# Two state-space layers on one core: gates between the convolution's products, bias as a weight row, other PSUM rooms, later weight loads

## The chip, the cores and the metric

The kernel runs on one core of one Trainium2 chip. The metric is the device time of one execution, in microseconds (us). The kernel before takes 1482.97 us, the median of three runs (1477.59 to 1486.76). A core has TensorE (PE in the profile), VectorE (DVE), ScalarE (ACT), GpSimd (POOL) and SyncE (SP). Each takes its own instructions in order and waits for the others by semaphores. All DMAs here but a few are issued by SP, one after another.

## The reference, cut to what matters

An image of 64x64 tokens with 96 channels goes through two layers. Each normalizes its input over groups (`_gn`), computes a branch and adds it to its input. The second layer reads (the first is built the same way, without a separate projection per direction):

```
xz = x @ in_proj_w.T                    # 96 -> 384
xin, z = jnp.split(xz, 2, axis=-1)      # 192 channels each
xc = conv 3x3, depthwise, SAME (xin)
u  = silu(xc + conv_b)
y  = four selective scans of u (rows and columns, both ways), summed
y  = layernorm(y)
y  = y * silu(z)                        # the gate
return y @ out_proj_w.T
```

The scan's recurrence is `h = h * exp(dt*A) + dt*u*B`, its output `sum over the states of h*C` plus `D*u`. Each layer has 192 channels and 16 states per channel.

## The kernel before, in words

The main loop (L1712 to L1746) runs over the two layers. It loads the layer's weights (`scan_weights`, L186, and L1714 to L1724), calls `head`, then the scans, then a tail which normalizes, gates, projects and adds. Layer 1's scans are `near_scans` (L267): there the state dies out so fast that short stretches suffice. A flag computed on the chip decides whether `far_scans` (L606, inside `tc.If`) has to run; in the profiled execution it didn't. Layer 2's scans are `scans` (L724); in the trace all their operations bear the line L738. Everything before their steady run is in `first` (L995).

The 192 channels are three tiles of 64. A tile lies on 128 partitions, as two halves: the upper 64 partitions hold the even groups of 512 tokens (8 image rows), the lower 64 the odd ones. So `u[T]` is 128x2048, and a chunk `c` (0 to 3) is 128x512. `HALF` names the two halves.

`head(l, xT, w)` (L1252) computes `u` and the gate. Its parts:

- *Normalization.* The statistics `st` of the input are aggregated (`bn_aggr`), averaged over groups by a product with `gav` (the results go to `small`, columns at the end of the PSUM tile `accs`), and turned into a factor `rs` and a `shift`. DVE scales the weights by `rs` into `ws`; nine tiny products of weights and `shift` (`offset`) give the bias of every channel, copied to `bias`.
- *In-projections.* `project(b, c)` makes the 128x512 of tile `b` and chunk `c` by two products of 64 columns of weights with 512 tokens. `padded` (L1323) copies it with ACT, bias added, into `pad[b]`, an image with a border of one pixel. `borders(b)` (L1330) is four DMAs on SP that fill the rows above and below each chunk from the other half (the halo).
- *Convolution.* The twelve pieces (3 tiles, 4 chunks) are split over the engines. PE does tile 2's chunks 0 to 2 (`tap_pe`, nine products with diagonal matrices into a sum `cp`). DVE does three pairs of chunks (`tap_dve`, nine multiply-adds of 128x1052 in PSUM; a sum has 1056 floats, and two of them stand alternately in `accs`, a tile of five PSUM banks). ACT multiplies (`tap_act`) and POOL adds (`tap_pool`) for three more chunks. `silu` (ACT) turns a finished sum into `u`.
- *Gates.* `gate01` multiplies 128 columns of weights at once, for tiles 0 and 1; `gated01` is the SiLU by ACT, followed by two DMAs of 128 KB, as a 128x512 result holds two tiles. `gate2` and `gated2` do tile 2, with one DMA of 256 KB. The results wait in DRAM (`szd`) until the tail.
- *Start of y.* `start_y` (L1249, POOL here) sets `y = ds * u`, six pieces of 128x1024.

The PSUM of in-projections, `cp` sums and gates is a pool of three rooms of one bank. The SBUF pool of the gate results `sz` has four buffers.

The order inside the head is written by hand: each step gets a due time (`at`, L1423 to L1473), and the steps are issued in order of these times. Instructions issued through the helper `Ordered` (recorded as L261 in the head) keep that order on their engine; those issued through `nc` may be moved by the compiler's scheduler. In the head's PE order the in-projections come first, then the 27 products of `cp`, then the twelve gate units. Between, the due times on ACT alternate pad copies, tap products and SiLUs:

```
        for c in range(3):
            for k in range(9):
                at(t + 0.9 * k, tap_pe, 2, c, k)
            t += 8.1
            at(t + 0.1, silu, 2, slice(HT * c, HT * (c + 1)), partial(whole, ("cp", c)))
        for g in range(8):
            at(t, gate01, g)
            at(t + 0.5, gated01, g)
            t += 0.5
```

On SP, layer 1's head has, besides halos and gate stores, layer 2's weights: five loads of `ipw`, `v`, `op`, and 44 of `scan_weights(1)` for its second pair of directions, issued from 37.64 us on (those of the first pair follow the near scans). After the head, layer 2's `first` has on POOL's queue the loads of `du` (`spread`, L947) and a share of the products `bT`; `pj` is its first product, `xd` its copy by ACT.

Of the kernel before, what the change touches and what calls it, by code (L numbers as in the profile page):

```python
# [9 lines left out]
F32 = mybir.dt.float32  # L10
BF16 = mybir.dt.bfloat16
AF = mybir.ActivationFunctionType
ALU = mybir.AluOpType
# [4 lines left out]
HW = 64  # L18
# [26 lines left out]
def two_ss2d_layers(  # L45
# [107 lines left out]
    xT = xp.enter_context(tc.tile_pool(name="xT0", bufs=1)).tile([DM, L], F32, name="xT0")  # L153
# [32 lines left out]
    def scan_weights(l):  # L186

        xw, dwb, am = [], [], []  # L190
        D = 1 + l
        for p in range(1 + l):
            lp = 2 * l + p
            w = swp.tile([128, 2, 3, NC], F32, tag=f"xw{p}", name=f"xw{lp}")
            v = swp.tile([128, 2, 3, 128], F32, tag=f"dwb{p}", name=f"dwb{lp}")
            e = swp.tile([128, 2, 3, NS + 1], F32, tag=f"ab{p}", name=f"ab{lp}")
            a = swp.tile([128, 2, 2, 3, NP], F32, tag=f"am{p}", name=f"am{lp}")
            nc.vector.memset(v[96:128, 0:D], 0.0)
            for d in range(D):
                r = slice(NB + RK * d, NB + RK * d + RK)  # L200
                rr = slice(RK * d, RK * d + RK)
                hi = slice(64 * d, 64 * d + 64)
                c0 = NB + 2 * RK + NS * d
                for half in HALF:
                    for to, of in ((slice(0, NC - NS), slice(0, NC - NS)), (slice(NC - NS, NC), slice(c0, c0 + NS))):
                        nc.sync.dma_start(
                            out=w[half, d, 0:2, to],
                            in_=xpw[lp, :, d, of].rearrange("(b p) c -> p b c", b=2),
                        )
                        nc.sync.dma_start(out=w[half, d, 2, to], in_=xpw[lp, hi, 2, of])  # L210
                    nc.sync.dma_start(
                        out=v[r, d, 0:2, half], in_=dtw[lp, rr, d, :].rearrange("r (b p) -> r b p", b=2)
                    )
                    nc.sync.dma_start(out=v[r, d, 2, half], in_=dtw[lp, rr, 2, hi])
                    for b, (of, q) in enumerate(((HALF[0], d), (HALF[1], d), (hi, 2))):
                        nc.sync.dma_start(
                            out=v[NC : NC + 1, d, b, half],
                            in_=alb[lp, of, q, NS : NS + 1].rearrange("p o -> o p"),
                        )
                    nc.sync.dma_start(  # L220
                        out=e[half, d, 0:2, :],
                        in_=alb[lp, :, d, :].rearrange("(b p) n -> p b n", b=2),
                    )
                    nc.sync.dma_start(out=e[half, d, 2, :], in_=alb[lp, hi, 2, :])
            xw.append(w)
            dwb.append(v)
            am.append((a, e, D))
        return xw, dwb, am
# [38 lines left out]
    def near_scans(weights):  # L267
# [5 lines left out]
        with ExitStack() as sc:  # L273
# [25 lines left out]
            )  # L299

# [278 lines left out]
            weights_of(1)  # L579
            for j in range(len(units)):  # L580
                if j > 1:
                    weights_of(j)
                if 0 < j < len(units) - 1:
                    operands(j + 1)
                scan(j)
                if j == 1:
                    reach()
                if j == 2:
                    reached()
                if j == 4:  # L590
                    sum_up(1)
                add(j)
                if j == 3:
                    sum_up(0)
# [129 lines left out]
    def scans(weights, pps, ready):  # L724
# [18 lines left out]
        with ExitStack() as sc:  # L743
# [251 lines left out]
            def first(  # L995
# [3 lines left out]
                parts = [delta(T) for T in range(3)]  # L999
                for h in range(2):  # L1000
                    project(h)
# [250 lines left out]
    def head(l, xT, w):  # L1252

        ipw_s, v, ds = w["ipw"], w["v"], w["ds"]
        with ExitStack() as sc:
# [16 lines left out]
            gm, rs, shift = gst[:, 2:3], gst[:, 5:6], gst[:, 6:7]  # L1272
            dve.bn_aggr(gst[:, 0:2], w["st"].rearrange("p a b -> p (a b)"))
            W2 = HW + 2
            accs = cvp.tile([128, 5 * HT], F32, name=f"accs{l}")
            small = accs[:, 4 * SR * W2 : 4 * SR * W2 + 8]
# [10 lines left out]
            ws = cv.tile([DM, 2 * DI], F32, name=f"ws{l}")  # L1287
            bias = cv.tile([128, 5], F32, name=f"bias{l}")
            dve.scalar_tensor_tensor(shift, gm, -1.0, rs, ALU.mult, ALU.mult)
            for cut in (slice(0, 64), slice(64, DI), slice(DI, 2 * DI)):  # L1290
                dve.tensor_scalar_mul(ws[:, cut], ipw_s[:, cut], rs)

            def offset(to, of, n):
                pe.matmul(
                    small[to, 2 + n : 3 + n], ipw_s[:, of : of + to.stop - to.start], shift,
                    start=True, stop=True,
                )

            for half in HALF:
                offset(half, 0, 0)  # L1300
            for n in (1, 2):
                for half in HALF:
                    offset(half, 64 * n, n)
            offset(slice(0, 128), DI, 3)
            for half in HALF:
                offset(half, DI + 128, 4)
            dve.tensor_copy(bias, small[:, 2:7])
# [3 lines left out]
            def room(name):  # L1311
                return cvp.tile([128, HT], F32, tag="in", name=name, bufs=3)

            def project(b, c):
                ps = live["in", b, c] = room(f"in{l}_{b}_{c}")
# [7 lines left out]
            def padded(b, c):  # L1323
                act.activation(
                    pad[b][:, c, 1 : SR + 1, 1 : HW + 1],
                    live.pop(("in", b, c)).rearrange("p (r w) -> p r w", w=HW),
                    AF.Identity, bias=bias[:, b : b + 1],
                )
# [11 lines left out]
            def gate01(g):  # L1340
                ps = live["z", g] = room(f"z{l}_{g}")
                pe.matmul(
                    ps, ws[:, DI : DI + 128], xT[:, g * 512 : (g + 1) * 512], start=True, stop=True
                )

            def gated01(g):
                c, h = divmod(g, 2)
                sz = cw.tile([128, HT], F32, tag="sz", name=f"sz{l}_{g}")
                act.activation(sz, live.pop(("z", g)), AF.Silu, bias=bias[:, 3:4])
                for b, half in enumerate(HALF):  # L1350
                    sp.dma_start(
                        out=szd[l][b, HALF[h], HT * c : HT * (c + 1)], in_=sz[half]
                    )

            def gate2(c):
                ps = live["z2", c] = room(f"z{l}_2_{c}")
                for h, half in enumerate(HALF):
                    g = 2 * c + h
                    pe.matmul(
                        ps[half], ws[:, DI + 128 : 2 * DI], xT[:, g * 512 : (g + 1) * 512],  # L1360
                        start=True, stop=True,
                    )

            def gated2(c):
                sz = cw.tile([128, HT], F32, tag="sz", name=f"sz{l}_2_{c}")
                act.activation(sz, live.pop(("z2", c)), AF.Silu, bias=bias[:, 4:5])
                sp.dma_start(out=szd[l][2, :, HT * c : HT * (c + 1)], in_=sz)
# [19 lines left out]
            def tap_pe(b, c, k):  # L1387
                if k == 0:
                    live["cp", c] = room(f"cp{l}_{b}_{c}")
# [6 lines left out]
            def tap_dve(n, b, c, k):  # L1396
                i, j = taps[k]
                o = i * W2 + j
                acc = accs[:, 2 * SR * W2 * (n % 2) :][:, 0 : 2 * SR * W2]
                live["acc", b, c] = acc.rearrange("p (c r w) -> p c r w", r=SR, w=W2)  # L1400
# [26 lines left out]
            for b, order in ((0, (2, 3, 1, 0)), (2, (3, 2, 1, 0)), (1, (3, 2, 1, 0))):  # L1427
                for c in order:
                    at(t, project, b, c)
                    at(t + 0.95, padded, b, c)  # L1430
                    t += 0.9
                at(t + 1.0, borders, b)
            for c in range(3):
                for k in range(9):
                    at(t + 0.9 * k, tap_pe, 2, c, k)
                t += 8.1
                at(t + 0.1, silu, 2, slice(HT * c, HT * (c + 1)), partial(whole, ("cp", c)))
            for g in range(8):
                at(t, gate01, g)
                at(t + 0.5, gated01, g)  # L1440
                t += 0.5
            for c in range(NCH):
                at(t, gate2, c)
                at(t + 0.9, gated2, c)
                t += 0.9
            t = 2.6
            for n, (b, c) in enumerate(((0, 2), (0, 0), (1, 0))):
                for k in range(9):
                    at(t, tap_dve, n, b, c, k)
                    t += 1.3  # L1450
                at(
                    t + 0.1, silu, b, slice(HT * c, HT * (c + 2)),
                    lambda b=b, c=c: live.pop(("acc", b, c))[:, :, :, 0:HW],
                )
            t = 7.4
            for b, c in ((2, 3), (1, 3), (1, 2)):
                for k in range(9):
                    at(t - 1.5, tap_act, b, c, k)
                    if k:
                        at(t, tap_pool, b, c, k)  # L1460
                        t += 1.3
                at(
# [363 lines left out]
```

## Time and profile before

| what | us |
|---|---|
| runs, median of 3 | 1482.97 |
| profiled execution, its own time | 1485.29 |
| its span | 1483.5 |
| head of layer 1, from `bn_aggr` to the first `nu` product | 18.7 to 83.5 |
| near scans, to DVE's last sum | 83.5 to 153.5 |
| tail of layer 1, to the first `bn_aggr` of layer 2 | 156.2 to 199.6 |
| head of layer 2, to the first `pj` product | 199.6 to 258.5 |
| layer 2's first DVE product `b*du` | 287.1 |

The mean TensorE clock granted is 0.932. How to read the profile: the page's first lines give each engine's busy time, its share of the span and the number of instructions. Then the span is cut into 40 slices, and each digit is a share in tenths. The chain is the work that ended last, followed back from the end, by engine and by line. A row of the timeline is start, duration, engine, line, operation, output <- input, shapes, count, and in brackets how long the engine had been idle and who released it; a row with a count over one spans several instructions. A row of the waits is who waited for whom: us in total, times, longest. An fp32 product is recorded as two passes, so `x54` is 27 products.

### The profile page before, as it was taken

Reading aid. Unit: us, or ns where it says so; the run is one execution under the profiler, and the core shown is the slowest. Engines: PE = TensorE matmul, PEld = TensorE weight load, DVE = VectorE, ACT = ScalarE, POOL = GpSimd, SP = SyncE. Lnnn points to the kernel's source line nnn. Section 1 sums busy time; section 2 is a strip of 40 time slices with the busy share of each in tenths; the row PEclk is TensorE's granted clock in tenths of the full one; section 3 lists DMA queues with packets and bytes.
Section 4 is the critical chain, followed back from the end, with each engine's and each line's share of the span. In section 5 each row is a group of like instructions: output and inputs, shape, how many; then the busy total and the mean of one; then the engine's idle time right before and its main releaser. Section 6 shows DMA issues by size and latency. Waiting matters only on the chain.

```text
span 1483.5 us, 17337 instructions
## 1 busy us (share of the span) xinstructions
PE 1222.3 (82%) x5047; PEld 480.5 (32%) x5047; DVE 1317.1 (89%) x909; ACT 1224.9 (83%) x2508; POOL 1205.4 (81%) x663
## 2 busy tenths in 40 slices
PE   6874879598888888888797989798988888886888
PEld 3333323233332323333333333333333333322333
DVE  4738576579999999999999999999999999999996
ACT  5765347679989988999999999999998889897873
POOL 1843018679999998989898989898989898989895
PEclk9965879689899999999999999999999999999999
DMA  3251522615352626262626262626262626262634
GB/s 109 45 123 26 145 50 61 160 31 124 77 136 65 146 65 149 57 157 58 145 57 144 58 144 59 143 59 143 59 142 59 142 59 150 61 147 67 146 87 127
DMA packets 85812, 147.70 MB, mean 100 GB/s; under 512 B 33692, under 2 KB 36956, under 8 KB 85612
## 3 DMA queue, kind: packets, MB, share of 16 engines
q1 hardware_dynamic: 84028, 143.96, 40.7%
q0 software_dynamic: 576, 1.57, 0.4%
q8 instruction: 41, 0.67, 0.2%
q10 hardware_dynamic: 1104, 0.98, 0.2%
q14 instruction: 63, 0.52, 0.1%
HBM read 80.85 MB, written 12.13 MB: 63 GB/s over the span
## 4 chain that ended last, share of the span: by engine, by line
DVE 30%; issue 23%; PE 10%; ACT 10%; POOL 7%; DMA 6%; SPq 2%; DVEq 0%; POOLq 0%; ACTq 0%
DVE h L738 19%; DVE b L738 8%; POOL hc L738 5%; ACT a L738 3%; PE ys L738 3%; ACT bT L738 2%; PE pj L738 2%; DMA cb<-C 2%; PE b L738 2%; SPq L738 2%; DVE accs L261 1%; DMA szt<-szd 1%; DMA xT<-xs 1%; DMA du<-su 1%; PE pd L738 1%
## 5 line engine op out<-in xcount | busy, mean ns | idle before, releaser
L738 POOL TENSOR_TENSOR hc<-h,cb 128x1024 f32<-128x1024 f32 x384 | 903.5, 2373 | 94.1 <-DVE h L738 41.5
L738 DVE TENSOR_TENSOR_SCAN h<-a,carry,b 128x1024 f32<-128x1024 f32 x288 | 664.6, 2337 | 26.2 <-PE b L738 3.5
L738 ACT ACTIVATE a<-dt,am 128x1024 f32<-128x1024 f32 x384 | 438.3, 1142 | 69.3 <-DVE h L738 63.2
L738 PE MATMUL ys<-hc,fold 128*64 128x512 f32 x1536 | 430.0, 639 | 0.3 <-POOL hc L738 0.2
L738 ACT ACTIVATE bT<-duT,BT 128x192 f32<-128x192 f32 x1012 | 387.3, 445 | 3.6 <-PE b L738 1.3
L738 PE MATMUL b<-ident,bT 128*128 128x128 f32 x1536 | 219.4, 286 | 26.4 <-DVE h L738 18.2
L738 DVE TENSOR_TENSOR b<-b,du 128x1024 f32<-128x1024 f32 x192 | 231.9, 1208 | 6.8 <-PE b L738 6.8
L738 DVE TENSOR_TENSOR_SCAN h<-a,b 128x1024 f32<-128x1024 f32 x96 | 216.3, 2278 | 12.7 <-POOL hc L738 2.5
L738 PE MATMUL b<-B,selh 96*128 96x512 bf16 x384 | 117.2, 387 | 131.4 <-DVE h L738 131.2
L738 PEld LDWEIGHTS b<-ident,bT 128*128 128x128 f32 x1536 | 174.4, 145 | 150.9 <-DVE h L738 90.8
L738 PEld LDWEIGHTS ys<-hc,fold 128*64 128x64 f32 x1536 | 77.7, 138 | 141.2 <-issue 106.2
L738 PEld LDWEIGHTS <-selh 96*128 96x128 bf16 x384 | 25.6, 98 | 258.7 <-DVE h L738 204.4
L261 POOL TENSOR_TENSOR tap<-tap,tap 128x512 f32<-128x512 f32 x48 | 61.0, 1273 | 47.8 <-ACT tap L261 45.0
L738 PE MATMUL pj<-u,xw 64*124 64x512 f32 x192 | 94.1, 635 | 1.9 <-DVE w L738 1.2
L261 DVE SCALAR_TENSOR_TENSOR accs<-pad,v,accs 128x1052 f32<-128x1052 f32 x48 | 63.3, 1319 | 12.7 <-DMA pad<-pad 6.3
L738 PE MATMUL ys<-y,ident 128*128 128x512 f32 (+1 forms) x120 | 61.2, 612 | 0.0
L738 ACT CAST B<-pj 96x512 bf16<-96x512 f32 (+2 forms) x96 | 54.9, 575 | 4.7 <-PE pj L738 4.7
L738 POOL TENSOR_TENSOR sp<-sp,ln 128x512 f32<-128x512 f32 x45 | 57.8, 1284 | 0.2
L738 POOL TENSOR_TENSOR ln<-ln,w 128x512 f32<-128x512 f32 x45 | 57.9, 1286 | 0.0
L738 POOL TENSOR_TENSOR su<-sp,u 128x512 f32<-128x512 f32 x45 | 57.7, 1282 | 0.0
L261 POOL MEMSET pad<- 128x40 f32 (+1 forms) x24 | 2.7, 170 | 67.0 <-DVE g L1524 51.1
L738 PE MATMUL pd<-xd,dwb 29*64 29x512 f32 x192 | 55.0, 646 | 0.0
(184 smaller groups left out, 1234.9 us busy)
## 6 DMA issues: line engine op xcount, KB each, us to landing
cb<-C SPq DMA_DIRECT2D x256, 256.0 KB
dt<-sp SPq DMA_DIRECT2D x192, 128.0 KB
du<-su SPq DMA_DIRECT2D x180, 128.0 KB
szt<-szd SPq DMA_DIRECT2D x24, 256.0 KB
szd<-sz SPq DMA_DIRECT2D x32, 128.0 KB
xT<-xs SPq DMA_DIRECT2D x8, 384.0 KB
szd<-sz SPq DMA_DIRECT2D x8, 256.0 KB
xs<-xT SPq DMA_DIRECT2D x1, 1536.0 KB
```

What stands on the lines that cost most here:

```text
L261: return lambda *args, **more: tc.keep_in_program_order(op(*args, **more))
L738: return lambda *args, **more: tc.keep_in_program_order(op(*args, **more))
```

## The change

1. `xT` gets a 97th row of ones (a POOL memset). The bias becomes the 97th row of the weights `ws`: one product of a 96x97 matrix `low` (zero but for its last column, the shift) with the weights, and a copy of one row. The nine `offset` products and the bias copy go. The pad copies are plain copies, two of the twelve by DVE.
2. The three rooms become two of one bank, by name: in-projections alternate by chunk, `cp` sums take room 0, gates room 1. DVE's sums get three banks of their own each, two of them.
3. Gates are twelve units (tile, chunk) of two products, each stored by one DMA of 256 KB; `sz` has eight buffers. The units stand between the `cp` products: 39 slots, nine of each thirteen for `cp`.
4. DVE, ACT and POOL do the first three taps of two pieces (the row that needs no halo) before the other taps of the first.
5. `start_y` moves from the head to the near scans (POOL, behind its memsets and `picked`) and to layer 2's `first`, ahead of POOL's `du` loads and `bT` products there.
6. Layer 2's `ipw`, `v`, `op` and the scan weights of its second pair of directions (49 DMAs) are issued in the near scans, behind the copies of `nS` on SP and ahead of its last loads `ab` and the branch. The sum `ds` of layer 2 goes with them (DVE).

```diff
-    xT = ....tile([DM, L], F32, name="xT0")
+    xT = ....tile([DM + 1, L], F32, name="xT0")
+    nc.gpsimd.memset(xT[DM : DM + 1], 1.0)
+    ones, xT = xT, xT[0:DM]
...
+    def layer_weights(l, queue):
+        w = {"st": st[l], "next": st[1]}
+        w["ipw"] = wts.tile([DM, 2 * DI], F32, name=f"ipw{l}")
+        queue.dma_start(out=w["ipw"], in_=ipw[l])
...
+        nc.vector.reduce_sum(w["ds"], v[:, :, V_D : V_D + 4], axis=AX.X)
+        return w
...
-    def near_scans(weights):
+    def near_scans(weights, later):
...
+            for start in later:
+                start()
...
             weights_of(1)
+            look_ahead()
...
                 parts = [delta(T) for T in range(3)]
+                for start in later:
+                    start()
                 for h in range(2):
                     project(h)
...
-            accs = cvp.tile([128, 5 * HT], F32, name=f"accs{l}")
-            small = accs[:, 4 * SR * W2 : 4 * SR * W2 + 8]
+            def room(name, tag):
+                return cvp.tile([128, HT], F32, tag=f"p{tag}", name=name)
+            small = room(f"pm{l}", 0)
...
-            for half in HALF:
-                offset(half, 0, 0)
...
-            dve.tensor_copy(bias, small[:, 2:7])
+            ws = cv.tile([DM + 1, 2 * DI], F32, name=f"ws{l}")
+            low = cv.tile([DM, DM + 1], F32, name=f"low{l}")
+            pool.memset(low, 0.0)
+            dve.scalar_tensor_tensor(low[:, DM:], gm, -1.0, rs, ALU.mult, ALU.mult)
+            offset = room(f"of{l}", 1)[0 : DM + 1, 0 : 2 * DI]
+            pe.matmul(offset, low, ipw_s, start=True, stop=True)
+            dve.tensor_scalar_mul(ws[0:DM], ipw_s, rs)
+            dve.tensor_copy(ws[DM:], offset[DM:])
...
-            def room(name):
-                return cvp.tile([128, HT], F32, tag="in", name=name, bufs=3)
...
-                act.activation(
+                copy = dve.tensor_copy if (b, c) in ((0, 2), (0, 1)) else act.copy
+                copy(
...
+            def gate(b, c):
+                ps = live["z", b, c] = room(f"z{l}_{b}_{c}", 1)
...
+                        ps[half], ws[:, DI + 64 * b : DI + 64 * b + 64],
+                        xT[:, g * 512 : (g + 1) * 512], start=True, stop=True,
...
+            def gated(b, c):
+                sz = cw.tile([128, HT], F32, tag="sz", name=f"sz{l}_{b}_{c}", bufs=8)
+                act.activation(sz, live.pop(("z", b, c)), AF.Silu)
+                sp.dma_start(out=szd[l][b, :, HT * c : HT * (c + 1)], in_=sz)
...
-                    live["cp", c] = room(f"cp{l}_{b}_{c}")
+                    live["cp", c] = room(f"cp{l}_{b}_{c}", 0)
...
+                if k == 0:
+                    live["acc", b, c] = cvp.tile(
+                        [128, 3 * HT], F32, tag="acc", name=f"acc{l}_{b}_{c}", bufs=2
+                    )[:, 0 : 2 * SR * W2]
...
+            for n in range(39):
+                c, k = divmod(n * 9 // 13, 9)
+                if n * 9 % 13 < 9:
+                    at(t, tap_pe, 2, c, k)
+                    if k == 8:
+                        at(t + 1.0, silu, 2, slice(HT * c, HT * (c + 1)), partial(whole, ("cp", c)))
+                else:
+                    z = n - (n * 9 // 13 + 1)
+                    at(t, gate, z // NCH, z % NCH)
+                    at(t + 0.95, gated, z // NCH, z % NCH)
+                t += 0.87
...
+            for b, c, k0, k1 in (
+                (0, 2, 0, 3), (0, 0, 0, 3), (0, 2, 3, 9), (0, 0, 3, 9), (1, 0, 0, 9)
+            ):
...
+            for b, c, k0, k1 in (
+                (2, 3, 0, 3), (1, 3, 0, 3), (2, 3, 3, 9), (1, 3, 3, 9), (1, 2, 0, 9)
+            ):
...
+    def look_ahead():
+        ahead["w"] = layer_weights(1, sp)
+        ahead["sw"] = scan_weights(1, 1, sp)
...
-        sw = scan_weights(l)
-        head(l, xT, w)
+        w = ahead.pop("w") if l else layer_weights(0, nc.sync)
+        sw = list(zip(*[scan_weights(l, 0, nc.sync)] + ([ahead.pop("sw")] if l else [])))
+        later = head(l, ones, w)
```

## The prediction

> **What bounds the kernel now.** I read the page first: busy shares, the 40 slices, the chain by engine and line.
>
> ```profile
> span 1483.5 us, 17337 instructions
> PE 1222.3 (82%) x5047; PEld 480.5 (32%) x5047; DVE 1317.1 (89%) x909; ACT 1224.9 (83%) x2508; POOL 1205.4 (81%) x663
> ...
> PEclk9965879689899999999999999999999999999999
> ...
> DVE 30%; issue 23%; PE 10%; ACT 10%; POOL 7%; DMA 6%; SPq 2%; DVEq 0%; POOLq 0%; ACTq 0%
> ```
>
> DVE sets the whole, but in layer 2's scans; the change doesn't touch those. The low clock digits lie in the first fifth, where the heads are, so I took the windows of the two heads, of head 0's gate stage, and of the steady scan.
>
> ```profile
> core 0: us, PE busy (x) PEld busy (x) DVE busy (x) ACT busy (x) POOL busy (x), PEclk, DMA share, GB/s
> 18.70:83.50 64.80, 56.31 (x157) 21.52 (x157) 37.54 (x38) 42.13 (x69) 41.93 (x29) 0.89 0.38 88
> 70.70:83.50 12.80, 9.73 (x21) 2.24 (x19) 0.00 (x0) 6.27 (x9) 11.58 (x6) 0.60 0.88 203
> 199.60:258.50 58.90, 52.38 (x157) 20.39 (x157) 37.46 (x37) 39.36 (x61) 36.98 (x27) 0.89 0.23 51
> 320.00:1440.00 1120.00, 952.40 (x4184) 361.13 (x4184) 1083.84 (x602) 1019.22 (x2144) 1040.94 (x514) 0.97 0.43 101
> ```
>
> Head 0 takes 64.8 us and head 1 58.9 us, and TensorE is the busiest in both. The 5.9 us between them lie in the second row: clock 0.60, DVE idle. The timeline shows why:
>
> ```profile
> 70.69 13.99 SPq L261 DMA_DIRECT2D szd<-sz  x20
> ...
> 73.80 0.69 ACT L261 ACTIVATE sz<-z,bias 128x512 f32<-128x512 f32 x1 [4.07 <-DMA szd<-sz]
> ...
> 74.54 9.01 PE L261 MATMUL z<-xT,ws 96*128 96x512 f32 x18 [3.07 <-ACT sz L261]
> ```
>
> The first gate was ready at 66.7, but its store was issued only at 70.69, since SP was at layer 2's 49 loads (37.64 to 70.69). With four `sz` buffers ACT stopped for 4.07 us; TensorE stopped behind it and came back at half rate. Head 1 has no such queue. From its timeline and table of waits:
>
> ```profile
> 220.16 24.96 PE L261 MATMUL cp<-pad,diag 128*128 128x512 f32 x54 [2.28 <-ACT pad L261]
> ...
> 258.50 3.80 PE L738 MATMUL pj<-u,xw 64*124 64x512 f32 x12
> ...
> 262.33 0.59 ACT L738 COPY xd<-pj 124x512 f32<-124x512 f32 x1 [0.38 <-PE pj L738]
> ```
>
> ```profile
> ACT sz L261 <- DMA szd<-sz: 3.6, 6, 0.8
> ...
> DVE accs L261 <- DMA pad<-pad: 3.3, 1, 3.3
> ...
> DVE accs L261 <- ACT u L261: 2.4, 2, 1.2
> ```
>
> TensorE goes from 204.08 to 258.50 and straight into layer 2's `pj`: this sets the end of the head. DVE's sums end at 250.88, so its two waits are off that path.
>
> **What the Trainium skill says.** "PSUM — Partial Sum Buffer", section "PSUM bank collisions raise a hardware error": two engines may not touch one bank (in the same partitions) at once, even at different columns, so they are ordered by bank. The trace agrees: a sum of 1056 floats reaches into the other's bank, and DVE waits 1.18 us twice for ACT's 1.11 us `u`. "TensorE: Matmul & The Clock Gate", Part 1: the array drops to half rate after an idle window of about 3.4 us. The trace shows the halves (0.86 against 0.43 us a pass), but an idle of 2.28 us already brought it (four passes of 0.86 from 220.16), while waits of 0.9 to 1.0 at 214.8 to 216.5 didn't; and after 3.07 us idle it stayed slow for 9 us. "SBUF — State Buffer", "Who interferes with whom": DVE with two SBUF inputs contends with GpSimd's reads, which bears on the moved `start_y`; layer 2's first DVE work lasted 0.69 us an instruction with GpSimd's `y` beside it (267.3 to 269) and without (271 on), so I charge nothing.
>
> **Part by part, in head 1's times.**
>
> *Bias as a weight row.* The 18 tiny passes (1.64 us) go; one product of 384 columns comes. Two passes at half rate, by the columns' ratio from 0.86: 0.64 each, 1.28, from about 202.7 to 204.0; then a row copy on DVE, 0.5 (0.56 for the 128x384 COPY). First `in` at 204.75 instead of 204.08: +0.67. The GpSimd memset of one row of 4096 isn't in the trace: from 128x384 at 0.42 and 32x768 at 0.73 I take 3.5 us (0.4 if elements across partitions counted, 7 at worst). It precedes the identity, which the transposes at 3.9 need; their next input lands at 7.1 and DVE's first statistics come at 12.3, so up to 7 is mostly hidden; kept at 0.
>
> *Two rooms instead of three for in-projections.* Freely running, TensorE would need 5.4 us for the slow start (204.08 to 209.5 now, 3.2 pairs) and 8.8 pairs at 0.86, and be through at 217.8. With two rooms it waits for the copies: about 1.0 at `in(0,1)`, and 1.65 behind `pad(2,3)`, where ACT also has tap products; through at about 220.4. `cp` takes the room of the last copy, `pad(1,0)`, while now it waited only for `pad(1,2)`: that copy ends about 222.3, so `cp` starts at 222.5 instead of 220.16: +2.3, the 0.67 in it.
>
> *Gates between the convolution's products.* 27 `cp` and 12 gate units at 0.86: 33.5 us. Now it is 27x0.86, 8x0.86 and 4x1.08 (the last paced by ACT), the half-rate start (+1.7) and waits (1.17, 0.44, 0.19, 0.26). New: all three `cp` sums share one room, so sums 2 and 3 each wait about 1.05 for the `u` before them (0.69 and two hand-overs, of which 1.17 is the sample). 222.5+33.5+2.1+0.3 = 258.4; up to 1.7 more if `cp` starts at half rate. So TensorE ends where it ended: what the denser order wins, the later start takes.
>
> *The end of the head.* `pj` takes the bank of the last `cp` sum and waits for its `u`, at 259.4 to 261.1; the second `xd` copy follows 3.8 us later (258.50 to 262.33 now): 263.2 to 264.9, +0.9 to +2.6. I take +1.9.
>
> *Whole stores, eight buffers.* 12 issues instead of 20; ACT's 3.6 us go. No gain beyond the above, since gates are now spread over 33 us.
>
> *Own banks for DVE's sums, first taps before the halo.* The 3.3 and 2.4 go, two pad copies of about 0.7 come: DVE ends near 247 instead of 250.9, GpSimd's sums stay near 252. Both lie under TensorE's 258: 0.
>
> *`start_y` moved.* Six GpSimd instructions of 2.84 us (17.06) now follow the head. In layer 2 they precede 12 `du` loads on GpSimd's queue (0.536 each, 6.4) and its four `bT` products. With last `u` at T, `y` ends T+17.1, the issues T+23.5; `bT` (284.82 now, T+26.3 moved) keeps 2 to 3 us, and the first `du` lands about 283 against its use at 289. Without this cover each further us costs one. In layer 1 `y` runs from 82 to 99; GpSimd's next use is at about 105: hidden by 6 us.
>
> *Layer 2's weights later.* The 49 loads (30.5 us without the halo among them, 0.62 each) move behind the near scans' `nS` copies and ahead of the last `ab` loads and SP's branch. SP starts them at about 111 and reaches the branch at 145; DVE's near work ends at 148 to 150 (153.48 now). Hidden by about 4; it becomes the bound if an issue costs over 0.71. Nobody in layer 1 waits for those `ab`. The small sum `ds` on DVE now stands among the near scans, behind a load that lands around its turn: +0.3.
>
> *Head 0* is the same walk 180.87 earlier: TensorE ends at 77.5 to 79.2, so the near products `nu` start 4.3 to 6.0 before 83.47: -5.1. They also start at full clock (now 4.2 us for 24 passes of 192 columns at half rate): -0.5 to -1.5, I take -0.7. With +0.3: -5.5.
>
> **Sum.** -5.5+1.9 = -3.6. The profiled execution's own time is 1485.29 (1.8 us around the span): 1481.7. The runs' median is 1482.97, so 1479.4 on that scale.
>
> **Rivals.** (A) *Both heads win.* TensorE stays at full rate through `cp`'s start, the `u` waits are covered by the gate units in between, and `pj` doesn't meet the last bank: head 1 -3, head 0 -8 with -1.5 in `nu`: -12.5, 1470.5. For: the waits of 0.9 that kept the clock. Against: one room for three sums. (B) *The other side: two rooms keep TensorE at half rate through the in-projections.* Place: `in` to `cp`. 12 pairs at 1.71 from 204.75 end 225.3, with the last waits `cp` starts at 226.9, +4.4 in each head: head 1 +6.3, head 0 -1.1, sum +5.2: 1488.2. It decides if the new waits reach the 2.28 us that brought half rate; at 1.0 they don't; 1.65 lies between. (C) *The 4.07 only moves:* ACT, TensorE or the `u` of GpSimd's sums (252) hold head 0 as before, or the branch waits for SP: sum about 0, 1483. (D) *SP or GpSimd becomes the bound:* with 0.9 us an issue SP is 44 us at it, 9 past DVE: +5.4 net, 1488; GpSimd's `y` slowed to 3.6 by DVE eats its slack and 2 us more.
>
> **Chances.** Forecast 0.48, own range 1474 to 1485 (the two ends of each term, +-2.5, and the runs' scatter of 9 us from 1477.6 to 1486.8). A 0.20, B 0.17, C 0.08, D 0.07. The range 1467 to 1491 takes in A and B with some scatter. About 1%, 14.8 us, is what a measurement of this kernel can tell from no change. Faster than 1468.1: a half of A and a little unforeseen, 0.13. Slower than 1497.8: the tails of B and D, 0.07. Same: 0.80.
>
> **What would show it.** In the changed profile: no `sz` wait for `szd` and `nu` at 77.5 to 79.5 (head 0's step); `cp` starting 2.3 later after the first `in` +0.7, with a clock digit that doesn't fall before it (against B); two waits of about 1 us of `cp` for `u`; `pj` behind the last `u`, second `xd` copy 0.9 to 2.6 later, measured from the head's `bn_aggr`; SP through with its loads before DVE's last near sum; `bT` on GpSimd not waiting for its own queue. I am wrong if TensorE's products between `cp` and the last gate take less than 33 us or more than 38, if the scan from 320 on changes its period, or if the near stage ends on SP.

## The result, and the profile after

The changed kernel takes 1497.79 us, median of 14 runs (1490.45 to 1506.71), against 1482.99 for the kernel before in its 14 runs (1477.59 to 1489.65): ratio 1.0096, 95% interval 1.0071 to 1.0121. (Ratios, here and below, are those on record for the runs, not quotients of the two medians.) It is slower by 10.5 to 18 us, where the forecast was 3.6 faster. The profiled execution (1506.71) is the longest of the 14, so I compare stages, and leave the end of layer 2's scans, which the change doesn't touch, for the last paragraph on the cause.

The page of the changed kernel:

```profile
span 1504.9 us, 17294 instructions
...
PE 1240.2 (82%) x5047; PEld 475.1 (32%) x5047; DVE 1323.0 (88%) x909; ACT 1215.3 (81%) x2504; POOL 1213.3 (81%) x667
...
PEclk8985979779889988999999999999999999999999
...
DVE 26%; issue 21%; PE 12%; POOL 11%; ACT 10%; DMA 6%; SPq 3%; DVEq 0%; POOLq 0%; ACTq 0%
```

PE and POOL have grown on the chain, DVE has shrunk, and the low clock digits are still there. The windows of the two heads, from `bn_aggr` to what follows, then two stretches inside head 1:

```profile
18.54:86.15 67.61, 59.74 (x156) 16.98 (x157) 38.63 (x37) 38.83 (x67) 32.06 (x27) 0.85 0.25 79
199.64:268.05 68.41, 59.89 (x156) 16.76 (x156) 39.55 (x38) 37.76 (x61) 30.50 (x24) 0.85 0.21 68
217.00:224.00 7.00, 5.00 (x20) 1.07 (x20) 6.82 (x7) 6.38 (x13) 4.78 (x5) 1.00 0.20 41
224.00:231.00 7.00, 6.99 (x10) 1.77 (x10) 6.86 (x6) 3.68 (x5) 4.55 (x4) 0.54 0.26 70
```

Head 0 has grown from 64.8 to 67.6 us, head 1 from 58.9 to 68.4. DMA is quiet (0.25 and 0.21): the store queue that stopped head 0 is gone, and something else has taken more. TensorE's timeline in head 1 shows what:

```profile
209.19 7.10 PE L271 MATMUL in<-xT,ws 97*64 97x512 f32 x20 [0.68 <-ACT pad L271]
217.11 3.94 PE L271 MATMUL in<-xT,ws 97*64 97x512 f32 x16 [0.82 <-ACT pad L271]
221.81 1.08 PE L271 MATMUL in<-xT,ws 97*64 97x512 f32 x4 [0.76 <-ACT pad L271]
224.01 1.56 PE L271 MATMUL cp<-pad,diag 128*128 128x512 f32 x2 [1.12 <-ACT pad L271]
225.50 1.98 PE L271 MATMUL z<-xT,ws 97*64 97x512 f32 x4
227.41 3.78 PE L271 MATMUL cp<-pad,diag 128*128 128x512 f32 x4
...
232.24 1.99 PE L271 MATMUL cp<-pad,diag 128*128 128x512 f32 x4
234.16 1.08 PE L271 MATMUL z<-xT,ws 97*64 97x512 f32 x4
235.17 1.98 PE L271 MATMUL cp<-pad,diag 128*128 128x512 f32 x4
...
240.85 1.13 PE L271 MATMUL cp<-pad,diag 128*128 128x512 f32 x2 [0.78 <-ACT u L271]
...
268.05 3.80 PE L751 MATMUL pj<-u,xw 64*124 64x512 f32 x12 [0.78 <-ACT u L271]
```

Three things are to be seen. In-projections wait for copies (0.68, 0.82, 0.76), the first `cp` product too (1.12), and the 5.00 busy of 7.00 us before `cp` is followed by half rate: two products of `cp` take 3.7 us (227.41 to 231.12) where the same two later take 1.9 (232.24 to 234.16). At full rate, two `cp` products and a gate take 2.92 to 2.93 us (232.24 to 235.17), not 2.58. The gate's weight load starts only with its product, at 234.16:

```profile
234.16 0.20 PEld L271 LDWEIGHTS z<-xT,ws 97*64 97x64 f32 x4 [0.76 <-ACT tap L271]
```

And `cp` waits for `u` between its sums, as does `pj` at the end.

The starts of such rows are the measure for all kernels below (us): the first `cp` product, the first product behind the head (`nu` in layer 1, `pj` in layer 2) and the second `xd` copy, each from the head's `bn_aggr`; and from the second `xd` copy to the second `b*du` of layer 2 ("first part").

| kernel | head 0: cp, nu | layer 2's bn_aggr | head 1: cp, pj, second xd | first part |
|---|---|---|---|---|
| before | 20.6, 64.8 | 199.6 | 20.6, 58.9, 62.8 | 32.3 |
| changed | 24.5, 67.6 | 199.6 | 24.4, 68.4, 72.3 | 34.0 |
| b_weights_later | 19.8, 57.9 | 194.2 | 20.5, 58.9, 62.7 | 31.8 |
| b_later_8 | 21.0, 57.4 | 193.0 | 20.7, 57.3, 61.1 | 33.1 |
| b_two_rooms | 21.1, 64.5 | 196.9 | 22.8, 61.2, 65.0 | 32.2 |
| a_wide | 24.1, 62.9 | 195.2 | 24.3, 64.1, 67.9 | 33.3 |
| a_gates_last | 24.7, 62.2 | 198.8 | 23.8, 63.7, 67.5 | 32.0 |
| a_y_order | 24.1, 65.6 | 198.2 | 24.3, 68.4, 72.2 | 32.0 |
| a_alternate | 20.9, 60.8 | 194.9 | 21.1, 62.0, 65.8 | 33.1 |
| a_swap | 24.7, 62.5 | 194.3 | 24.3, 66.3, 70.1 | 34.1 |
| a_three_rooms | 18.2, 56.0 | 187.4 | 18.7, 56.6, 60.5 | 33.0 |
| a_all | 18.5, 55.2 | 188.2 | 19.1, 55.1, 58.9 | 32.3 |
| a_all_own | 21.3, 56.7 | 189.4 | 21.1, 57.4, 61.3 | 32.1 |
| a_all_taps | 22.1, 59.6 | 191.5 | 22.3, 60.1, 63.9 | 32.7 |

The ten heads with the change's rooms and order of in-projections (changed, a_wide, a_gates_last, a_y_order, a_swap) start `cp` at 23.8 to 24.7, so a shift of more than one us there is not scatter. Behind `cp`, the clock of the single execution moves a head by up to 3.2 us; where that enters a comparison, it is said.

### The profile page after: what moved, and what is told of

The parts are those of the page before. It is cut to its first block, busy times and chain, and to the rows that moved or that the text cites. A ratio compares the mean times of both kernels' runs of the same rounds, so it can differ in the third digit from the quotient of the medians.

```text
span 1504.9 us, 17294 instructions
## 1 busy us (share of the span) xinstructions
PE 1240.2 (82%) x5047; PEld 475.1 (32%) x5047; DVE 1323.0 (88%) x909; ACT 1215.3 (81%) x2504; POOL 1213.3 (81%) x667
## 4 chain that ended last, share of the span: by engine, by line
DVE 26%; issue 21%; PE 12%; POOL 11%; ACT 10%; DMA 6%; SPq 3%; DVEq 0%; POOLq 0%; ACTq 0%
DVE h L751 16%; DVE b L751 8%; POOL hc L751 7%; ACT a L751 3%; DMA cb<-C 3%; PE pj L751 3%; ACT bT L751 2%; PE ys L751 2%; SPq L751 2%; PE cp L271 2%; PE b L751 2%; POOL sp L751 2%; DMA szt<-szd 2%; POOL ln L751 1%; DMA dt<-sp 1%
## 5 line engine op out<-in xcount | busy, mean ns | idle before, releaser
L751 PE MATMUL b<-ident,bT 128*128 128x128 f32 x1536 | 224.9, 289 | 36.3 <-DVE h L751 19.9
L751 PEld LDWEIGHTS b<-ident,bT 128*128 128x128 f32 x1536 | 177.9, 147 | 163.0 <-DVE h L751 89.9
L751 PE MATMUL pj<-u,xw 64*124 64x512 f32 x192 | 98.9, 663 | 3.6 <-ACT B L751 1.2
L271 DVE SCALAR_TENSOR_TENSOR acc<-pad,v,acc 128x1052 f32<-128x1052 f32 x48 | 62.9, 1318 | 1.5
L271 PE MATMUL cp<-pad,diag 128*128 128x512 f32 x108 | 58.8, 664 | 5.3 <-ACT u L271 3.1
L751 POOL TENSOR_TENSOR sp<-sp,ln 128x512 f32<-128x512 f32 x45 | 57.9, 1286 | 0.2
L751 PEld LDWEIGHTS pj<-u,xw 64*124 64x124 f32 x192 | 35.0, 197 | 63.5 <-issue 48.6
```

The costliest lines, as they stand in the source:

```text
L271: return lambda *args, **more: tc.keep_in_program_order(op(*args, **more))
L751: return lambda *args, **more: tc.keep_in_program_order(op(*args, **more))
```

## The experiments

Kernels named a_ are the changed one with an edit, those named b_ the one before with an edit. My theory after the two traces was that TensorE's stage in the heads had been mis-sized: by the switches between gates and `cp`, and by the rooms. The rivals were the interleaving as such, the moved `start_y`, and that the later loads had brought nothing.

**b_weights_later**: part 6 alone.

```diff
...
-        sw = scan_weights(l)
+        w = ahead.pop("w") if l else layer_weights(0, nc.sync)
+        sw = list(zip(*[scan_weights(l, 0, nc.sync)] + ([ahead.pop("sw")] if l else [])))
```

> The kernel before with part 6 alone (layer 2's 49 loads behind the near scans' nS copies). The prediction's step for head 0: the 4.07 us wait of ACT for its gate stores goes and the gates run at full clock, so from bn_aggr to the first nu product 64.8 becomes 59 to 61; head 1 stays at 62.8 from bn_aggr to the second xd copy; whole kernel -4 to -5 us. Rival (the stall only moves, to the stores' own queue or to the near scans): nu earlier by less than 1 us or the tail of layer 1 no earlier, whole kernel 0.

Measured: 1480.84 against 1485.61, ratio 0.9963 (0.9933 to 0.9992). `nu` starts 6.9 us earlier after `bn_aggr` (57.9, where 59 to 61 was expected), and the near scans give 2.6 back. Layer 2's `bn_aggr` is 5.4 earlier, but 0.9 of that lies before head 0's own `bn_aggr` (17.75 instead of 18.69): 4.5 is gained between the two. About 1.5 of the 6.9 is not the loads' doing: the first 7 us from `cp` ran at full clock here and at 0.78 before, after the same wait of 2.3 us. In head 0's table of waits ACT's 4.07 is gone:

```profile
ACT sz L269 <- DMA szd<-sz: 3.6, 6, 0.7
```

Six short waits remain, none over 0.7, as head 1 always had them. The prediction's step for the loads stands as to the stall; in the changed kernel other steps ate it.

**a_wide**: gates of tiles 0 and 1 at 128 columns, still interleaved.

```diff
+                if b < 2:
+                    g = NCH * b + c
...
+                    pe.matmul(
+                        ps, ws[:, DI : DI + 128], xT[:, g * 512 : (g + 1) * 512],
...
```

> The changed kernel, with the gates of tiles 0 and 1 as products of 128 columns of weights (eight units, stored in two DMAs each) still between the convolution's products. Theory of the switch: going from a 64-column product to a 128x128 one and back costs TensorE 0.34 us a unit (period of two cp products and a gate 2.92 instead of 2.58), since the next weights aren't loaded ahead; then eight of twelve units lose it, head 1 from bn_aggr to the second xd copy 72.3 becomes 69.5, kernel -5 in both heads. Rival, that the interleaving itself (hand-over of the one gate room to ACT, whatever the width) makes the period 2.92: no change, 72.3.

Measured: second `xd` 67.9 instead of 72.3; 1489.38 against 1485.61, ratio 1.0040 (1.0019 to 1.0061). Its timeline of TensorE:

```profile
224.79 1.02 PE L271 MATMUL z<-xT,ws 97*128 97x512 f32 x2
225.65 1.88 PE L271 MATMUL cp<-pad,diag 128*128 128x512 f32 x4
227.37 1.02 PE L271 MATMUL z<-xT,ws 97*128 97x512 f32 x2
```

From gate to gate 2.58 us, with the same single room and the same hand-over to ACT: the rival is out, and the 0.34 belongs to the change of width. Eight units make 2.7 of the 4.4; about 1.5 is a shorter half-rate start of `cp` in this execution (clock 0.76 in its first 7 us instead of 0.54).

**a_gates_last**: the twelve units behind the 27 products (`if n < 27: tap_pe ... else: gate`), in two rooms by turns.

> The changed kernel with the twelve gate units behind the 27 convolution products (PE order of before), in two alternating rooms. Theory of the switch: 3.7 us less of cp-and-gates (12 x 0.34, less the switch that stays), also no pj behind the last u; but cp sums 2 and 3 still wait for their room and gates wait for ACT: head 1 72.3 becomes 67 to 69. Rival, that the late and half-rate start of cp (two rooms) is all the loss: 72 stays.

Measured: 67.5; 1491.52, ratio 1.0049 (1.0027 to 1.0071). The number is in the expected range, in part by luck: of the 4.8 us, 0.6 is an earlier `cp` and 1.6 its clock (0.77 in the first 7 us instead of 0.54). What is left, 2.6, is less than the 12 changes of width and the wait of `pj` come to together. The late `cp` (23.8) stays.

**a_y_order**: `start_y` in the order in which `u` is ready.

```diff
-                for b, c in ((2, 2), (0, 2), (1, 2), (2, 0), (0, 0), (1, 0))
+                for b, c in ((0, 2), (0, 0), (1, 0), (1, 2), (2, 0), (2, 2))
```

> The changed kernel with start_y's six pieces in the order of their u: those of the last cp sum at the end. GpSimd now idles 8.9 us for the first piece, then its 17.7 us of y, its du loads and its bT products follow. Theory that this queue costs the 1.8 us that layer 2's first part lost (34.0 instead of 32.3 from the second xd copy to the second b*du) and more behind cover: that part becomes 32 or less, head 1 the same 72.3, kernel -2. Rival, that GpSimd isn't on the path and half-rate TensorE is: 34 stays.

Measured: first part 32.0 instead of 34.0, head 1 unchanged, both as expected; 1495.07, ratio 1.0054 (1.0032 to 1.0075). GpSimd's timeline in the changed kernel shows what was cured:

```profile
268.10 17.72 POOL L271 TENSOR_SCALAR y<-u,ds 128x1024 f32<-128x1024 f32 x6 [8.85 <-ACT u L271]
285.76 4.30 POOL L751 DMA_DIRECT2D du<-su  x8
290.57 0.52 POOL L751 DMA_DIRECT2D du<-su  x1 [0.50 <-DVE duT L751]
292.60 0.52 POOL L751 DMA_DIRECT2D du<-su  x1 [1.51 <-DMA du<-su]
...
296.01 2.98 POOL L751 TENSOR_SCALAR bT<-duT,BT 128x192 f32<-128x192 f32 x4
```

The queue held for the one `u` that came last, then the late `du` loads waited for earlier ones to land, and the `bT` products stood behind them; TensorE waited 3.75 us for the first. In all five kernels with gates between the products and the old order of `y` (changed, a_wide, a_alternate, a_swap, a_three_rooms) the second `b*du` starts 10.6 us after the first; in the other nine it is 6.8 to 7.6.

**b_two_rooms**: `bufs=3` to `bufs=2` in the kernel before.

> The kernel before with two rooms instead of three, the same instructions. Theory of the rooms: the first cp product starts 20.6 us after bn_aggr in the kernel before and 24.4 in the changed one; 0.7 of the 3.8 is the bias row (first in-projection 5.2 instead of 4.5), the rest is the second room's wait and the longer half-rate start; so here cp starts at 23 to 24 with in at 4.5, in both heads. Rival, that ACT's order of taps and copies in the changed kernel makes it late: cp stays at 20.6 to 21.5.

Measured (a single run, 1482.46): `cp` at 21.1 and 22.8, by 0.5 and 2.2 later; less than the theory said, and in head 0 what the rival said. Two rooms in strict turn cost something, but not 3.

**a_three_rooms**: rooms and banks as in the kernel before, all else changed.

```diff
-                return cvp.tile([128, HT], F32, tag=f"p{tag}", name=name)
+                return cvp.tile([128, HT], F32, tag="in", name=name, bufs=3)
...
```

> The changed kernel with three rooms shared by in-projections, cp sums and gates, and DVE's sums again side by side in five banks. Theory of the rooms: cp starts at 21.3 to 22 instead of 24.4, sums 2 and 3 don't wait for the u before them (2 us), pj doesn't wait for the last u; the 64-column switches stay: from bn_aggr to the second xd copy 72.3 becomes 66 to 67.5. DVE's bank waits of 1.2 us come back and cost nothing. Rival, that the switches and ACT are all of it: 71 or more.

Measured (a single run, 1474.42): second `xd` 60.5 and `nu` 56.0, more than expected, and below the kernel before. From TensorE's timeline and the windows of head 1:

```profile
192.68 13.40 PE L271 MATMUL in<-xT,ws 97*64 97x512 f32 x48 [0.66 <-DVE ws L271]
206.10 1.13 PE L271 MATMUL cp<-pad,diag 128*128 128x512 f32 x2
...
243.99 3.80 PE L751 MATMUL pj<-u,xw 64*124 64x512 f32 x12
```

```profile
206.00:213.00 7.00, 6.98 (x20) 2.04 (x18) 6.82 (x6) 6.97 (x13) 6.12 (x6) 1.00 0.35 90
```

All twelve in-projections run without a wait in one row, `cp` follows at once at full clock (1.00 where the changed kernel had 0.54), and `pj` follows the last `cp` product. Rooms and banks together cost the changed kernel 11.8 us in head 1 and 11.6 in head 0. The 11.8 can be taken apart: 5.6 until `cp`, 3.2 the half-rate start (7 us at 0.54), 2.1 the two waits for `u` between the sums, 0.8 the wait of `pj`.

**a_alternate**: two rooms, but in turn.

```diff
-                ps = live["in", b, c] = room(f"in{l}_{b}_{c}", c % 2)
+                ps = live["in", b, c] = room(f"in{l}_{b}_{c}", len(made) % 2)
```

> The changed kernel with its two rooms taken strictly in turn by the in-projections. In the change the room follows the chunk, and in the order 2, 3, 1, 0 the second and third product use one room, in the order 3, 2, 1, 0 it alternates. With three rooms cp started at 18.7 instead of 24.4 us after bn_aggr in head 1 and 18.2 instead of 24.5 in head 0. If the doubled room is what makes it late: cp at 20 to 21.5. If the number of rooms is (each product waits for the copy two before it, while ACT has taps between): 23 to 24.5. The second xd copy moves with it, 67.5 to 69 or 71 to 72.3.

Measured (a single run, 1486.56): `cp` at 20.9 and 21.1. Of the 5.6 us that rooms cost until `cp` in head 1, 3.2 are the room that two products in a row shared, 2.4 the missing third. With the earlier `cp` came a start at full clock (1.00 instead of 0.54 for 7 us, 3.2 us): `xd` is at 65.8, 6.5 us earlier, twice the gain at `cp` and more than either expectation.

**a_swap**: `cp` sums in alternating rooms, gates in the other one.

```diff
-                    live["cp", c] = room(f"cp{l}_{b}_{c}", 0)
+                    live["cp", c] = room(f"cp{l}_{b}_{c}", c % 2)
...
-                ps = live["z", b, c] = room(f"z{l}_{b}_{c}", 1)
+                ps = live["z", b, c] = room(f"z{l}_{b}_{c}", 1 - turn[0] % 2)
```

> The changed kernel with the three cp sums in alternating rooms and the gates always in the other. The first cp of sums 2 and 3 then doesn't wait for the u of the sum before it (0.8 us of TensorE idle each, 1.6 with the late weight load); the gate one product later may wait for the rest. If that wait counts: second xd copy 1.0 to 1.7 earlier (70.6 to 71.3). pj still waits for the last u. If it only moves to the gate: 72 stays.

Measured (a single run, 1484.29): `xd` at 70.1, 2.1 earlier, where 1.0 to 1.7 was expected. The clock behind `cp` is the same in both (0.54). The three products across the end of a sum, up to the next gate, take 2.78 us here (232.72 to 235.50) and 3.82 in the changed kernel (238.09 to 241.91). Each of the two waits thus costs 1.04, of which TensorE is idle for 0.78; they count in full.

**a_all**: three rooms, wide gates, `start_y` in order; **a_all_own**: the same mending with two rooms, in turn and swapped, and DVE's own banks.

> The changed kernel with the three suspected causes undone at once: three rooms and shared banks, gates of tiles 0 and 1 at 128 columns, start_y in the order of its u. If the causes add up: cp at 21.3 to 22, second xd copy 62 to 63.5 after bn_aggr, second b*du 32 later, head 1 as in the kernel before (62.8), head 0 shorter by 5; kernel 1478 to 1482 where before is 1485, that is -4 to -7. If something else of the change costs too: head 1 stays above 65.

> The changed kernel with its own banks for DVE's sums kept, so two rooms, and everything else mended: rooms in turn, cp sums in alternating rooms, gates of tiles 0 and 1 at 128 columns, start_y in the order of its u. With three rooms and shared banks such a kernel had its second xd copy 58.9 after bn_aggr and took 1467.6. If two rooms are no worse once they alternate: 59 to 61 and 1468 to 1472. If the third room is worth what the in-projections show: 63 to 66, 1476 to 1481. DVE's own banks (2.4 us of its waits) bring nothing in either.

Measured: a_all 1467.57 against 1485.33, ratio 0.9896 (0.9848 to 0.9944); a_all_own 1474.96 against 1484.66, ratio 0.9936 (0.9910 to 0.9961). a_all beats both kernels, and by more than expected: `xd` is at 58.9 instead of 62 to 63.5, as three rooms alone had already given 60.5 instead of 66 to 67.5. The single gains are not a plain sum: one at a time, the rooms brought 11.8 at `xd` and the wide gates 4.4; together they bring 13.4, in part because both gains contain the same half-rate start. Where it is absent on both sides, the wide gates bring 1.5 (60.5 to 58.9), less than eight times 0.34. a_all_own lies between its two expectations. Own banks bring nothing that three rooms don't: `xd` 61.3 against 58.9.

**b_later_8**: the later loads and eight gate buffers in the kernel before.

> The kernel before with part 6 (loads later) and eight gate buffers instead of four. The waits of ACT for gate stores (3.6 us in head 1 in six pieces) go; the last gate SiLU, which delays the first xd copy, comes earlier by 1 us: second xd copy 61.5 to 62.3 after bn_aggr instead of 62.8; head 0 as with the later loads alone (nu 57.9) or 0.5 less; kernel -5 to -6 against before.

Measured: 1480.51, ratio 0.9971 (0.9950 to 0.9993). `xd` is 1.7 earlier, a little more than expected, but the first part 0.9 longer, and the whole is no better than with four buffers (1480.84), a little short of the 5 to 6 expected.

**a_all_taps**: a_all with ACT's and GpSimd's taps in the order of before.

```diff
-                (2, 3, 0, 3), (1, 3, 0, 3), (2, 3, 3, 9), (1, 3, 3, 9), (1, 2, 0, 9)
+                (2, 3, 0, 9), (1, 3, 0, 9), (1, 2, 0, 9)
...
```

> The kernel of the mended version (three rooms, wide gates, start_y in order) with ACT's and GpSimd's taps in the order of the kernel before: all nine of a piece before the next, so that the fourth waits for the halo. In the kernel before ACT waits 2.25 us there with pad copies queued behind it, and the first cp product waits 2.28 for such a copy. With three rooms and the new order cp started at 18.5 and 19.1 after bn_aggr, in spite of the bias row, against 20.6 before. If the new order of taps is why: cp at 20.5 to 21.5 here, second xd copy 60.5 to 61.5 instead of 58.9. If the two pad copies by DVE are why: cp stays at 18.5 to 19.3.

Measured (a single run, 1476.80): `cp` at 22.1 and 22.3 instead of 18.5 and 19.1, `xd` 5.0 later. Its table of waits in head 1:

```profile
ACT tap L271 <- DMA pad<-pad: 2.8, 1, 2.8
...
PE in L271 <- ACT pad L271: 2.8, 1, 2.8
```

ACT stands at the halo, the pad copies queue behind it, and TensorE stands 2.8 us for a room. Both shifts are larger than expected. In the 7 us from `cp` the clock is 0.65 instead of 1.00 (2.4 us), enough for the rest of the 5.0. So the new order of taps is why a_all starts `cp` early; the two pad copies by DVE, which stay, are not.

## Why the prediction was wrong, step by step

The forecast was off by 14.9 us in stages: +11.3 where -3.6 was forecast. Of this 5.6 lie before layer 2's `bn_aggr` (head 0, -5.5 forecast, +0.1 measured), 7.6 in head 1 (+1.9 and +9.5) and 1.8 in layer 2's first part. By its steps:

*Two rooms for in-projections* is the first that failed. It put `cp` at +2.3; measured +3.8 and +3.9. Its working was wrong in three places. It took the rooms as alternating, and missed that `c % 2` gives chunks 3 and 1 the same room (3.2 us, a_alternate). It measured against 20.6, though without the room shortage this code starts `cp` at 18.7. And it read the clock's limit from waits that were not TensorE's: the "waits of 0.9 to 1.0" that kept the clock are those of the weight loads, while the products ran through in one row and stood still for at most 0.11 us:

```profile
204.08 13.80 PE L261 MATMUL in<-xT,ws 96*64 96x512 f32 x48
...
214.76 0.20 PEld L261 LDWEIGHTS in<-xT,ws 96*64 96x64 f32 x4 [0.90 <-ACT pad L261]
...
215.94 0.20 PEld L261 LDWEIGHTS in<-xT,ws 96*64 96x64 f32 x4 [0.99 <-ACT pad L261]
```

So no wait near 1.0 had been seen to be harmless. In the changed kernel none exceeded 1.12; the clock halved behind them for 7.0 us, where "up to 1.7" had been allowed. Nor is this a fixed price. The ten heads named under the table have the same 5.00 of 7.00 us busy before `cp`; in the 7 us from `cp` the clock was 0.54 in four of them, 0.76 or 0.77 in four and 1.00 in two. One of the two is head 0 of a_swap:

```profile
36.04:43.04 7.00, 5.00 (x20) 1.07 (x20) 6.83 (x6) 6.38 (x13) 4.78 (x5) 1.00 0.18 38
43.04:50.04 7.00, 7.00 (x20) 2.14 (x22) 6.86 (x6) 5.56 (x9) 5.59 (x5) 1.00 0.32 93
```

Over the ten heads it costs 2.0 us in the mean (7 us times the missing share of the clock). That the profiled execution met the dear case, 3.2, in both heads is bad luck. The 2.28 of before is no limit either: in b_weights_later `cp` of head 0 came after 2.29 us idle and ran at 1.00.

*The first taps before the halo* were costed at 0, with DVE's sums as the reason. The reason held for DVE; but the edit also moved ACT's taps, and ACT's halo wait had pad copies behind it that TensorE needed. a_all_taps prices it, with three rooms, at 3.2 to 3.5 us until `cp` and 5.0 at `xd`. What it is worth with the change's two rooms was not tried.

*Gates between the products* had 33.5 + 2.1 + 0.3 and up to 1.7 from `cp` to the last product, 35.9 to 37.6. Measured 43.0 (224.01 to 265.29 and 1.72): past the 38 that it had named as a sign of being wrong. It is made of the same 33.5; two waits for `u` of 1.04 each, as predicted; 12 changes of width and back at 0.34, 4.1 where 0.3 stood; and the half-rate start, 7.0 x 0.46 = 3.2, in this execution. The profile of before has no 64-column product between two of 128; such a gap asks for a bound from both sides, and I gave it the price of the uniform rows alone.

*The end of the head* was right: `pj` waits for the last `u`, and the second `xd` follows 3.8 us after it. *The bias row* was right: +0.67 (head 1) and +0.78 (head 0).

*`start_y`* was costed at 0 with 2 to 3 us of cover. `y` ended at T+17.8, about as thought, but the `du` loads took until T+28 instead of T+23.5, and the cover was gone: 1.8 us (a_y_order takes back 2.0). The working gave them 12 issues without a wait; before, they had taken 8.7 us (270.86 to 279.55), in groups with gaps between. The other half of this step, nothing for GpSimd's `y` beside DVE, rested on a few instructions that were not lengthened. In the changed kernel one was, to 1.49 us from 0.69:

```profile
277.25 1.49 DVE L751 TENSOR_TENSOR wl<-wl 128x512 f32<-128x512 f32 x1
```

In nine of the fourteen kernels such an instruction is lengthened at this place, each time while `y` runs. It shows no cost here, since the second `b*du` waits for GpSimd's `bT`.

*Later loads, head 0*: right as to the stall. By themselves they bring -4.5 from one `bn_aggr` to the next in b_weights_later, with -5.5 forecast for the whole change; the parts agree less (6.9 until `nu`, 1.5 of it clock, and 2.6 lost again in the near scans, for which no run gives the cause). In the changed kernel the same TensorE stage put `nu` at 67.6, 7.9 behind the forecast's 59.7. The near scans then took 2.0 us less than before; 1.4 of it is their last sum, which waited 1.66 instead of 3.02 for TensorE. *SP* was through at 152.0, before DVE's last near sum at 154.1, so the look-ahead was hidden, with 2 us to spare instead of 4; the memset of a row of ones took 3.51, as estimated.

Of the rivals, B named the place (two rooms, `in` to `cp`, half rate) but thought of the in-projections themselves, and priced it at +5; the fault came at `cp`. A's argument, the waits of 0.9 that kept the clock, rested on the same misreading. D's queue of GpSimd came in small.

What stays open: stages give +11.3, the medians +14.8 with an interval that holds it. In the profiled execution layer 2's scans after the second `b*du` took 1199.0 us against 1188.9, but in the twelve edited kernels, with the same scans, they took 1183.7 to 1199.4. Part of it can be seen: `b*du` falls behind by 4.3 us at one place, where TensorE has half its clock. The windows of changed and before there, 11.4 us apart:

```profile
418.00:429.00 11.00, 11.00 (x25) 3.85 (x23) 7.92 (x4) 6.13 (x14) 11.00 (x8) 0.55 0.36 96
```

```profile
406.60:417.60 11.00, 10.83 (x44) 4.26 (x43) 10.73 (x6) 9.83 (x23) 11.00 (x8) 1.00 0.36 96
```

The Trainium skill, "TensorE: Matmul & The Clock Gate", section "What's actually happening", says that the clock's activity window runs freely and does not start with the kernel, so that its phase differs between executions. That agrees with this scatter, and with the ten heads that met the same waits at three different clocks; that it is the cause of either was argued here, not tried.

## What to carry to other kernels

Before PSUM rooms are taken away from a pipeline, write down for each product which copy it waits for and what its engine has queued ahead of that copy; waits of 0.8 to 1.1 us in a row can cost more than their sum, since in eight of ten heads TensorE ran at half rate behind them for a while. Before a wait is called harmless, see in the trace whether the products waited or only the weight loads. Interleave products only at one width of weights, or count the price of each excursion, 0.34 us here. When an edit is costed at nothing, name every engine that it moves work on: here the same edit was idle for DVE and worth 3 us through ACT in a_all.

## What the runs showed of the hardware that was not expected

A TensorE change from a 128-column product to a pair of 64-column products and back costs 0.34 us: the weight load, which otherwise runs ahead by 0.43 us (at 235.27 for the pass at 235.70), starts with the product (both at 234.16). Half rate can follow a stretch of short waits (5.00 of 7.00 us busy, no wait over 1.12 us), for 7 us, for about half of that, or not at all; behind the eight heads of a_alternate, a_three_rooms, a_all and a_all_own, with 5.38 us or more of the 7.00 busy, the clock stayed at 1.00. Single DVE instructions of 0.69 us took up to 1.65 (`wl`, a_all) while GpSimd's `y` ran. GpSimd's last `du` loads waited up to 1.51 us for earlier ones when all twelve were issued in a row; the traffic was as dense before (227 GB/s against 223), where they came in groups and one waited 0.33.
